# Long convolutions around a Haar perceptron layer: whole-width transfers, an earlier threshold, and C's start inside A's end

## The chip, the cores and the metric

The kernel runs on one core of a Trainium2 chip. The metric is the device time of one execution in microseconds; the kernel before took 3163.57 us (median of 3 runs, 3160.73 to 3165.43). The engines are PE (TensorE, matrix multiplication into PSUM), DVE (VectorE), ACT (ScalarE), POOL (GpSimd, which works on SBUF here) and SP (SyncE, whose queue issues every DMA of this kernel). Each engine works through its own queue in order, and waits on semaphores for the others.

## The reference, cut to what matters

The input `x` is 4 images of 64 channels of 256 x 256, in float32. Four layers follow one another:

```
x  = conv(x, filters of L0)        # two-dimensional causal long convolution, plus x * bias
f1 = haar2d(x)                     # all eight levels, along both axes
for i in 0, 1:
    f4   = einsum(f1 * v[i], conv_w[i])             # mixes the 64 channels, point by point
    acc += sign(f4) * relu(abs(f4) - tau[i])        # soft threshold
x  = haar2d_inverse(acc) + x
x  = conv(x, filters of L2)
x  = conv(x, filters of L3)
```

The filter of a convolution is the outer product of two filters of 256 taps, one along each axis, that a small network of sines makes. So a convolution is a multiplication with a triangular Toeplitz matrix along the rows and one along the columns.

## The kernel before, in words

**Three phases.** Phase A does the first convolution and the Haar transform, channel by channel. Phase B mixes the channels and applies the soft threshold, row of coefficients by row. Phase C undoes the transform and does the last two convolutions, again channel by channel. Between them the data lies in HBM: A writes `coef`, B reads it and writes `mixed`, C reads that. The four images are worked through as two groups of two. B of a group needs all channels of A; C of a group needs all rows of B.

**Phase A** has 32 rounds a group, each of two channels, so four images a round. A round has 12 pieces: four of `rows` (PE lines 223 and 224, then a copy on ACT, L292), four of `columns` (PE, then bias and addition on DVE, L302), and four of `product` for the round before (PE L317, the Haar transform along one axis, evicted by ACT, L325). The transform along the other axis is a row of small additions and subtractions on POOL (L241 and L244), of which two are issued with a piece. `coarsest` (L331 to L333) finishes two coefficients and `store` (L339) writes `coef`. Loads of `x` (L104) and of the Toeplitz matrices (L215) are issued two rounds ahead.

**Phase B** has 64 steps a group. A step is one row of each of the two halves of the 128 coefficient rows: 64 channels of one row on partitions 0 to 63, 64 channels of the other on partitions 64 to 127. `load` issues, for each half, one DMA for `f` (L392), one for `v` (L396) and one for `tau` (L397), each to 64 partitions; `store` (L455) writes each half with a DMA. In the first step of a group three DVE operations (L449 to L451) turn a pair of the first row into sum and difference. A step has two units `u`, one for each of the two terms of the sum. A unit does:

- `mix`: two multiplications of 128 x 512 on PE (L409) into a PSUM tile `f4`, of which there are two; `mix_sb` holds the channel weights twice, on its diagonal
- `multiply`: f4 times v, on DVE (L413)
- `sign` of f4 into an SBUF tile `m`, on ACT (L417), and `magnitude`, f4 = |f4|, on ACT (L420)
- `less`: f4 minus tau, on DVE (L424)
- `threshold`: max(f4, 0) times m, on DVE (L429)
- `add`: the even unit's term to `f` on POOL (L434), the odd unit's to that on POOL (L440) or, in every second step, on DVE (L438), which then reads f4

The pieces of B are written so that unit `u` and unit `u - 1` overlap: piece 0 has `mix(u)` and `less(u - 1)`; piece 1 has `multiply(u)`, `sign(u)`, then `threshold(u - 1)` and `add`; piece 2 has `magnitude(u)`.

**Phase C** has 32 rounds a group of 20 pieces: `product` (PE L522, ACT L526), `rows` and `columns` of two convolutions (PE lines 223 and 224, ACT L533, DVE L546). Before a round, POOL makes the inverse sums (L264 and L266) from the loaded `mixed`.

**The order of the work** is written out by hand: there is no scheduler, and instructions go into the queues in the order of the calls. `beside(main, side, lead, tail)` (L585) calls the pieces of `main` and spreads those of `side` evenly between them, from piece `lead` to `tail` pieces before the end. First A's first group runs with the filter network beside it; then A's second group with B's first (lead 20, tail 4), C's first group with B's second (lead 8, tail 40), and C's second group alone. C's round 0 loads, sums and filters are issued inside C's piece 0 (L559 to L564), after all of A.

Of the kernel before, what the change touches and what calls it, by code (L numbers as in the profile page):

```python
# [29 lines left out]
F32 = mybir.dt.float32  # L33
AF = mybir.ActivationFunctionType
ALU = mybir.AluOpType
# [30 lines left out]

@with_exitstack
def conv_haar_kernel(
    ctx: ExitStack, tc: tile.TileContext, x, zT, w1, wbd, cols, decay, bias, haarW, haarH, wcol, wrow, mixT, v, tau, out
):  # L70
    nc = tc.nc
    ctx.enter_context(tc.manual_schedule())
# [123 lines left out]
    bias_sb = const.tile([P, NL * C], F32, tag="bias", name="bias_sb")  # L196
    nc.sync.dma_start(bias_sb, bias.partition_broadcast(P))
    mix_sb = const.tile([P, 2, P], F32, tag="mix", name="mix_sb")
    nc.gpsimd.memset(mix_sb, 0.0)
    for i in range(2):  # L200
        for g in range(2):
            s = slice(g * C, (g + 1) * C)
            nc.sync.dma_start(mix_sb[s, i, s], mixT[i])

    def load_toeplitz(l, t, bufs):

# [68 lines left out]
    def phase_a():  # L275


        total = GROUPS * ROUNDS
        st = [dict() for _ in range(total + 1)]
        pieces = []  # L280

        def load(t):
            if t < total:
                st[t]["x"] = first_x[t] if t < len(first_x) else load_x(t)
                st[t]["toep"] = load_toeplitz(0, t, 4 * CI)

        def rows(t, n):
            s = st[t]
            ps = bank(f"a1ps{n}_{t}")
            toeplitz(ps, s["x"][:, 2 * n : 2 * n + 2], s["toep"][n // NB], 0)  # L290
            s["y", n] = image("t0", f"ay{n}_{t}")
            nc.scalar.copy(s["y", n], ps)  # L292

        def columns(t, n):
            s = st[t]
            c = t % ROUNDS * CI + n // NB
            if n == 0:
                s["x1"] = big("m0", f"x1_{t}", 2)
            ps = bank(f"a2ps{n}_{t}")
            toeplitz(ps, s["y", n], s["toep"][n // NB], 1)  # L300
            cut = slice(2 * n, 2 * n + 2)
            nc.vector.scalar_tensor_tensor(  # L302
                s["x1"][:, cut], s["x"][:, cut], bias_sb[:, c : c + 1], ps, ALU.mult, ALU.add
            )
            if n == M - 1:
                s["fw"] = big("m1", f"fw_{t}", 2)
                s["ops"] = forward_free(s["x1"], s["fw"], f"f{t}_")

        def product(t, j):
            s = st[t]  # L310
            n, m = j // 2 * 2, j % 2
            if j == 0:
                s["f"] = big("out", f"f_{t}", 2)
            ps = bank(f"a3ps{j}_{t}")
            for e in range(2):
                for k in range(2):
                    nc.tensor.matmul(  # L317
                        ps[:, e, bass.ts(k, P)],
                        s["fw"][:, 2 * (n + e) + k, bass.ts(m, P)],
                        haarH_sb[:, k, :],  # L320
                        start=True,
                        stop=True,
                    )
            f4 = s["f"].rearrange("p (n m) k -> p n m k", m=2)
            nc.scalar.activation(f4[:, n : n + 2, m, :], ps, AF.Copy, scale=wcol_sb[:, m : m + 1])  # L325

        def coarsest(t):

            pairs = st[t]["f"].rearrange("p n (h q) -> p n h q", h=2)[:, :, :, 0]
            sd = ac.tile([P, 2 * M, 2], F32, tag="sd", name=f"sd_{t}", bufs=2)  # L330
            nc.gpsimd.tensor_tensor(sd[:, :, 0], pairs[:, :, 0], pairs[:, :, 1], ALU.add)  # L331
            nc.gpsimd.tensor_tensor(sd[:, :, 1], pairs[:, :, 0], pairs[:, :, 1], ALU.subtract)
            nc.gpsimd.tensor_copy(pairs, sd)  # L333

        def store(t):
            grp, c0 = t // ROUNDS, t % ROUNDS * CI
            for e in range(CI):
                src = st[t]["f"][:, 2 * e * NB : 2 * (e + 1) * NB].rearrange("p (b h) k -> p b h k", h=2)
                nc.sync.dma_start(coef[grp][c0 + e], src)  # L339
            st[t].clear()  # L340

        def piece(t, j):
            now, last = t < total, t > 0
            if j == 0:
                if t == 0:
                    load(0)
                    load(1)
                load(t + 2)
            if j < M:
                if now:  # L350
                    rows(t, j)
                if last:
                    run(st[t - 1]["ops"], 2)
            elif j < 2 * M:
                if now:
                    columns(t, j - M)
                if j == M and t > 1:
                    coarsest(t - 2)
                if j == M + 2 and t > 1:
                    store(t - 2)  # L360
            else:
                if last:
                    product(t - 1, j - 2 * M)
                if now:
                    run(st[t]["ops"], 2)

        for t in range(total + 1):
            for j in range(3 * M):
                pieces.append(lambda t=t, j=j: piece(t, j))
        pieces.append(lambda: (coarsest(total - 1), store(total - 1)))  # L370
        return pieces

    def phase_b(grp):

# [5 lines left out]
        def load(s):  # L380
            if s >= STEPS:
                return
            d = st[s]
            r0 = s * ROWS
            d["f"] = bp.tile([P, ROWS, NB, W], F32, tag="ft", name=f"ft_{grp}_{s}", bufs=4)
            d["v"] = bp.tile([P, ROWS, 2, W], F32, tag="v", name=f"v_{grp}_{s}", bufs=3)
            d["tau"] = bp.tile([P, ROWS, 2, W], F32, tag="tau", name=f"tau_{grp}_{s}", bufs=3)
            for g in range(2):
                part = slice(g * C, (g + 1) * C)
                rows = slice(g * C + r0, g * C + r0 + ROWS)  # L390
                flat = lambda ap: ap.rearrange("r i h k -> (r i h k)").partition_broadcast(C)
                nc.sync.dma_start(  # L392
                    d["f"][part].rearrange("p r b w -> p (r b w)"),
                    coef[grp][:, rows].rearrange("c r b h k -> c (r b h k)"),
                )
                nc.sync.dma_start(d["v"][part].rearrange("p r i w -> p (r i w)"), flat(v[rows]))  # L396
                nc.sync.dma_start(d["tau"][part].rearrange("p r i w -> p (r i w)"), flat(taus[rows]))  # L397

        def data(t):
            return t.rearrange("p r b w -> p (r b) w")  # L400
# [41 lines left out]
        def store(s):  # L442
            r0 = s * ROWS
            gt = st[s]["g"]
            if r0 == 0:

                top = gt[:C, 0].rearrange("p b (h k) -> p b h k", h=2)
                sd = bp.tile([C, NB, 2, N], F32, tag="sd", name=f"sd_{grp}", bufs=1)
                nc.vector.tensor_tensor(sd[:, :, 0, :], top[:, :, 0, :], top[:, :, 1, :], ALU.add)  # L449
                nc.vector.tensor_tensor(sd[:, :, 1, :], top[:, :, 0, :], top[:, :, 1, :], ALU.subtract)  # L450
                nc.vector.tensor_copy(top, sd)  # L451
            for g in range(2):
                part = slice(g * C, (g + 1) * C)
                rows = slice(g * C + r0, g * C + r0 + ROWS)
                nc.sync.dma_start(  # L455
                    mixed[grp][:, rows].rearrange("c r b h k -> c (r b h k)"), gt[part].rearrange("p r b w -> p (r b w)")
                )
            st[s].clear()

        def piece(u, j):  # L460
            s, i = divmod(u, 2)
            if j == 0:
                if u < units:
                    mix(u)
                if 0 < u <= units:
                    less(u - 1)
            elif j == 1:
                if u < units:
                    multiply(u)
                    sign(u)  # L470
                if 0 < u <= units:
                    threshold(u - 1)
                    add((u - 1) // 2, 1 - i)
                if i == 0 and s >= 2:
                    store(s - 2)
                    load(s + 2)
            elif u < units:
                magnitude(u)
# [11 lines left out]
    def phase_c():  # L490
# [65 lines left out]
        def piece(t, j):  # L556
            stage, n = divmod(j, M)
            if j == 0:
                if t == 0:  # L559
                    load(0)  # L560
                    load(1)
                    sums(0)
                    run(st[0]["ops"], 16)
                    filters(0)  # L564
                filters(t + 1)
                load(t + 2)
                sums(t + 1)
# [8 lines left out]
            if t + 1 < total:  # L576
                run(st[t + 1]["ops"], 1)

        for t in range(total):
            for j in range(5 * M):  # L580
                pieces.append(lambda t=t, j=j: piece(t, j))
        pieces.append(lambda: store(total - 1))
        return pieces

    def beside(main, side, lead, tail):  # L585

# [5 lines left out]
                q()  # L592
            done = max(done, want)

    a, c = phase_a(), phase_c()
    cut_a, cut_c = ROUNDS * 3 * M, ROUNDS * 5 * M
    beside(a[:cut_a], rest, 2, 3 * M)
    early.close()
    bp = pool("b", 2)
    bps = pool("bps", 2, space=PSUM)  # L600
    beside(a[cut_a:], phase_b(0), 5 * M, M)
    beside(c[:cut_c], phase_b(1), 2 * M, 10 * M)
    beside(c[cut_c:], [], 0, 0)


# [99 lines left out]
```

## Time and profile before

| | |
|---|---|
| median of 3 runs | 3163.57 us |
| profiled execution | 3161.11 us, its span 3159.3 us |
| PE | 2973.0 us, 94% of the span |
| DVE | 1564.9 us, 50% |
| ACT | 1230.2 us, 39% |
| POOL | 1817.4 us, 58% |
| DMA, all queues | 656.76 MB, mean 208 GB/s |
| granted PE clock | 0.989 |

The profile is of one execution. Its span goes from the first instruction to the last. A row of its windows gives the busy time of each engine in a stretch of the span, with the number of instructions in brackets. A row of its waits gives the waiting instruction, what released it, the idle time in total, how often, and the longest. A row of its timeline gives start, duration, engine, line, operation, the tile written and the tiles read, and in brackets the idle time before it with what ended it. B's first multiply starts at 533.3 us, the last of its first group at 1306.15, C's first product at 1342.91, and B's last multiply near 2300.6. A's rounds without B beside them are 14.06 us apart (products at 506.35 and 520.41), and C's without B 24.53 us.

### The profile page before, as it was taken

To read this page: it belongs to the slowest core of one execution; us is meant where nothing else is said; L and a number is where in the kernel's file an instruction comes from. 1 tells how busy PE (TensorE), PEld (TensorE's weight loads), DVE (VectorE), ACT (ScalarE), POOL (GpSimd) and SP (SyncE) were. 2 spreads that over 40 slices of the span, in tenths; PEclk is the share of its full clock that TensorE was granted. 3 is DMA by queue.
4 is the path that set the end of the run, shared out by engine and by line. 5 is a ranking of instruction groups with operands and counts; after the bars stand their busy time and mean duration, and the time that the engine had idled before them with its cause. 6 is when DMAs were issued, how large, how long until landed. Compare 5 with 4: busy or idle time off the path is not lost. (4 is left out here: it accounts for less than half of the span.)

```text
span 3159.3 us, 48195 instructions
## 1 busy us (share of the span) xinstructions
PE 2973.0 (94%) x17432; PEld 2535.1 (80%) x17432; DVE 1564.9 (50%) x1657; ACT 1230.2 (39%) x1799; POOL 1817.4 (58%) x2437
## 2 busy tenths in 40 slices
PE   5999999888988888599999999999999999999999
PEld 5989997666666666488877878887899999999998
DVE  2232213777777777457666667666732222222222
ACT  1333333444544445344444444444432222232222
POOL 2776675666766766655556555565664444444441
PEclk9999999999999999899999999999999999999999
DMA  6857898999999999789888988989744444444442
GB/s 159 215 179 193 226 234 226 258 274 272 274 275 270 274 277 265 230 195 268 233 244 226 250 231 238 249 226 255 205 141 132 141 124 124 124 138 132 127 120 87
DMA packets 380227, 656.76 MB, mean 208 GB/s; under 512 B 42134, under 2 KB 281399, under 8 KB 379992
## 3 DMA queue, kind: packets, MB, share of 16 engines
q1 hardware_dynamic: 379992, 653.69, 76.6%
q8 instruction: 140, 2.29, 0.3%
q14 instruction: 95, 0.78, 0.1%
HBM read 438.10 MB, written 215.42 MB: 207 GB/s over the span
## 5 line engine op out<-in xcount | busy, mean ns | idle before, releaser
L409 PE MATMUL f<-ft,mix_sb 128*128 128x512 f32 x1024 | 506.1, 617 | 112.6 <-DVE gt L438 57.3
L434 POOL TENSOR_TENSOR m<-m,ft 128x1024 f32<-128x1024 f32 x128 | 301.7, 2357 | 453.1 <-DVE m L429 441.4
L417 ACT ACTIVATE m<-f 128x1024 f32<-128x1024 f32 x256 | 262.5, 1025 | 513.1 <-DVE f L413 504.3
L546 DVE SCALAR_TENSOR_TENSOR cy<-cz,bias_sb,c1c 128x512 f32<-128x512 f32 x256 | 189.2, 746 | 515.9 <-PE c1c L224 515.9
L424 DVE TENSOR_TENSOR f<-f,tau 128x1024 f32<-128x1024 f32 x256 | 314.6, 1229 | 197.0 <-ACT f L420 194.2
L302 DVE SCALAR_TENSOR_TENSOR x<-x,bias_sb,a2ps 128x512 f32<-128x512 f32 x256 | 189.0, 745 | 428.8 <-PE a2ps L224 380.4
L409 PEld LDWEIGHTS f<-ft,mix_sb 128*128 128x128 f32 x1024 | 177.5, 193 | 258.3 <-issue 142.6
L546 DVE SCALAR_TENSOR_TENSOR o<-cy,bias_sb,c2c 128x512 f32<-128x512 f32 x256 | 189.5, 746 | 348.7 <-PE c2c L224 348.7
L413 DVE TENSOR_TENSOR f<-f,v 128x1024 f32<-128x1024 f32 x256 | 313.8, 1226 | 54.9 <-PE f L409 51.8
L223 PE MATMUL a1ps<-toep,x 128*128 128x256 f32 x1024 | 310.1, 385 | 21.3 <-DMA toep<-filt 18.1
L223 PE MATMUL a2ps<-toep,ay 128*128 128x256 f32 x1024 | 305.9, 381 | 1.8 <-ACT ay L292 1.8
L223 PE MATMUL c2r<-toep,cy 128*128 128x256 f32 x1024 | 305.8, 380 | 0.3 <-DVE cy L546 0.3
L223 PE MATMUL c1c<-toep,ch 128*128 128x256 f32 x1024 | 305.8, 380 | 0.0
L223 PE MATMUL c1r<-toep,cz 128*128 128x256 f32 x1024 | 305.8, 380 | 0.0
L223 PE MATMUL c2c<-toep,ch 128*128 128x256 f32 x1024 | 305.8, 380 | 0.0
L533 ACT COPY ch<-c2r 128x512 f32<-128x512 f32 x256 | 149.4, 588 | 382.4 <-PE c2r L224 382.2
L325 ACT ACTIVATE f<-a3ps,wcol_sb 128x512 f32<-128x512 f32 x256 | 175.7, 686 | 293.2 <-PE a3ps L317 251.5
L317 PEld LDWEIGHTS a3ps<-haarH_sb,fw 128*128 128x128 f32 x2048 | 244.9, 195 | 32.5 <-issue 22.7
L526 ACT COPY cz<-c1ps 128x512 f32<-128x512 f32 x256 | 148.1, 588 | 309.5 <-PE c1ps L522 309.5
L522 PEld LDWEIGHTS c1ps<-haarW_sb,ci 128*128 128x128 f32 x2048 | 238.8, 193 | 36.6 <-POOL ci L266 24.4
L522 PE MATMUL c1ps<-haarW_sb,ci 128*128 128x128 f32 x2048 | 244.6, 276 | 23.4 <-POOL ci L266 23.3
L420 ACT ACTIVATE f<-f 128x1024 f32<-128x1024 f32 x256 | 263.9, 1031 | 0.0
(64 smaller groups left out, 5868.5 us busy)
## 6 DMA issues: line engine op xcount, KB each, us to landing
toep<-filt SPq DMA_DIRECT2D x768, 128.0 KB, 4.1
x<-in_x SPq DMA_DIRECT2D x256, 256.0 KB, 7.8
coef<-f SPq DMA_DIRECT2D x128, 512.0 KB, 7.3
ft<-coef SPq DMA_DIRECT2D x256, 256.0 KB, 6.6
v<-in_v SPq DMA_DIRECT2D x256, 256.0 KB, 7.0
tau<-taus SPq DMA_DIRECT2D x256, 256.0 KB, 7.0
mixed<-gt SPq DMA_DIRECT2D x256, 256.0 KB, 6.0
g<-mixed SPq DMA_DIRECT2D x128, 512.0 KB, 5.4
```

The source lines that it names most:

```text
L223: nc.tensor.matmul(ps[:, m, :], data[:, 0, cut], t[:, which, :], start=True, stop=False)
L302: nc.vector.scalar_tensor_tensor(s["x1"][:, cut], s["x"][:, cut], bias_sb[:, c : c + 1], ps, ALU.mult, ALU.add)
L317: nc.tensor.matmul(ps[:, e, bass.ts(k, P)], s["fw"][:, 2 * (n + e) + k, bass.ts(m, P)], haarH_sb[:, k, :], start=True, stop=True,)
L325: nc.scalar.activation(f4[:, n : n + 2, m, :], ps, AF.Copy, scale=wcol_sb[:, m : m + 1])
L409: nc.tensor.matmul(un[u]["f4"][:, j, :], mix_sb[:, u % 2, :], f[:, j, :], start=True, stop=True)
L413: nc.vector.tensor_tensor(f4, f4, weights(st[u // 2]["v"], u % 2), ALU.mult)
L417: nc.scalar.activation(un[u]["m"], un[u]["f4"], AF.Sign)
L420: nc.scalar.activation(un[u]["f4"], un[u]["f4"], AF.Abs)
L424: nc.vector.tensor_tensor(f4, f4, weights(st[u // 2]["tau"], u % 2), ALU.subtract)
L434: nc.gpsimd.tensor_tensor(m0, m0, data(st[s]["f"]), ALU.add)
L522: nc.tensor.matmul(ps[:, m, bass.ts(h, P)], s["ci"][:, 2 * n + h, bass.ts(m, P)], haarW_sb, start=True, stop=True)
L546: nc.vector.scalar_tensor_tensor(o, s["y", n], bias_sb[:, at : at + 1], ps, ALU.mult, ALU.add)
```

## The change

There are four edits.

1. Each step of B loads `f`, `v` and `tau` and stores its result with one DMA over all 128 partitions, in place of one per half. For that the two halves are interleaved: partition 2c + g holds channel c of half g. `mix_sb` is laid out accordingly by the host and loaded whole, without a memset. The first row of a group is now on every second partition, so its three operations run on all partitions, with a factor (`first_sb`) that is 1 and -1, or 0 and 1, by partition.
2. In a unit of B, `threshold(u - 1)` and `add` stand right behind `less(u - 1)` in piece 0, so in front of `multiply(u)` in DVE's queue; before they stood behind it.
3. A's last round is taken out of its list: the products of the last round, with what POOL still has to do for them, form `a_last`, whose four products are placed between the first four `rows` of C.
4. B's first group is spread over A's second group up to six stages (24 pieces) before its end, where it went on to the end before. C's loads, filters and first sums of round 0 are issued in those 24 pieces. B's second group starts at piece 20 of the list that C leads, where it was piece 8.

```diff
-            for g in range(2):
-                part = slice(g * C, (g + 1) * C)
-                rows = slice(g * C + r0, g * C + r0 + ROWS)
-                flat = lambda ap: ap.rearrange("r i h k -> (r i h k)").partition_broadcast(C)
-                nc.sync.dma_start(
-                    d["f"][part].rearrange("p r b w -> p (r b w)"),
-                    coef[grp][:, rows].rearrange("c r b h k -> c (r b h k)"),
-                )
-                nc.sync.dma_start(d["v"][part].rearrange("p r i w -> p (r i w)"), flat(v[rows]))
-                nc.sync.dma_start(d["tau"][part].rearrange("p r i w -> p (r i w)"), flat(taus[rows]))
+            nc.sync.dma_start(d["f"].rearrange("p r b w -> p (r b w)"), rows_of(coef[grp], r0))
+            for name, src in (("v", v), ("tau", taus)):
+
+                flat = bass.AP(src.tensor, src.offset + r0 * 2 * W, [[0, C], [C * 2 * W, 2], [1, ROWS * 2 * W]])
+                nc.sync.dma_start(d[name].rearrange("p r i w -> p (r i w)"), flat)
+
+        def rows_of(ap, r0):
+            return ap.rearrange("c (g r) b h k -> c g r (b h k)", g=2)[:, :, r0 : r0 + ROWS].rearrange(
+                "c g r e -> c g (r e)"
+            )
...
-            for g in range(2):
-                part = slice(g * C, (g + 1) * C)
-                rows = slice(g * C + r0, g * C + r0 + ROWS)
-                nc.sync.dma_start(
-                    mixed[grp][:, rows].rearrange("c r b h k -> c (r b h k)"), gt[part].rearrange("p r b w -> p (r b w)")
-                )
+                top, low = (gt[:, 0].rearrange("p b (h k) -> p b h k", h=2)[:, :, h, :] for h in range(2))
+                d = bp.tile([P, NB, N], F32, tag="sd", name=f"sd_{grp}", bufs=1)
+                one, sign_ = first_sb[:, 0:1], first_sb[:, 1:2]
+                nc.vector.tensor_scalar(d, top, one, None, ALU.mult)
+                nc.vector.scalar_tensor_tensor(top, low, one, top, ALU.mult, ALU.add)
+                nc.vector.scalar_tensor_tensor(low, low, sign_, d, ALU.mult, ALU.add)
+            nc.sync.dma_start(rows_of(mixed[grp], r0), gt.rearrange("p r b w -> p (r b w)"))
...
                 if 0 < u <= units:
                     less(u - 1)
+                    threshold(u - 1)
+                    add((u - 1) // 2, 1 - i)
             elif j == 1:
                 if u < units:
                     multiply(u)
                     sign(u)
-                if 0 < u <= units:
-                    threshold(u - 1)
-                    add((u - 1) // 2, 1 - i)
...
-        for t in range(total + 1):
+        for t in range(total):
             for j in range(3 * M):
                 pieces.append(lambda t=t, j=j: piece(t, j))
-        pieces.append(lambda: (coarsest(total - 1), store(total - 1)))
-        return pieces
+        t = total - 1
+        last = [lambda: (coarsest(t - 1), store(t - 1), run(st[t]["ops"], 16))]
+        last += [lambda j=j: product(t, j) for j in range(M)]
+        last.append(lambda: (coarsest(t), store(t)))
+        return pieces, last
...
+        def start():
+            load(0)
+            load(1)
+            filters(0)
+            sums(0)
+
+        first = [start] + [lambda: run(st[0]["ops"], 2)] * 8
...
-    beside(a[cut_a:], phase_b(0), 5 * M, M)
-    beside(c[:cut_c], phase_b(1), 2 * M, 10 * M)
+    beside(a[cut_a : -6 * M], phase_b(0), 5 * M, 0)
+    beside(a[-6 * M : -2 * M], c_first[:1], 2 * M, M)
+    beside(a[-2 * M :], c_first[1:], 0, 0)
+    main = a_last[:1] + c[:M]
+    for pair in zip(c[M : 2 * M], a_last[1:]):
+        main += pair
+    main += a_last[M + 1 :] + c[2 * M : cut_c]
+    beside(main, phase_b(1), 5 * M, 10 * M)
     beside(c[cut_c:], [], 0, 0)
```

More of the change, by code (lines that the diff above doesn't have):

```diff
@@ L68, in conv_haar_kernel @@
 def conv_haar_kernel(
-    ctx: ExitStack, tc: tile.TileContext, x, zT, w1, wbd, cols, decay, bias, haarW, haarH, wcol, wrow, mixT, v, tau, out
+    ctx: ExitStack, tc: tile.TileContext, x, zT, w1, wbd, cols, decay, bias, haarW, haarH, wcol, wrow, mixT, first, v, tau, out
 ):
@@ L198, in conv_haar_kernel @@
     mix_sb = const.tile([P, 2, P], F32, tag="mix", name="mix_sb")
-    nc.gpsimd.memset(mix_sb, 0.0)
-    for i in range(2):
-        for g in range(2):
-            s = slice(g * C, (g + 1) * C)
-            nc.sync.dma_start(mix_sb[s, i, s], mixT[i])
+    nc.sync.dma_start(mix_sb, mixT)
+    first_sb = const.tile([P, 2], F32, tag="first", name="first_sb")
+    nc.sync.dma_start(first_sb, first)
     def load_toeplitz(l, t, bufs):
@@ L342, in piece @@
         def piece(t, j):
-            now, last = t < total, t > 0
             if j == 0:
@@ L349, in piece @@
             if j < M:
-                if now:
-                    rows(t, j)
-                if last:
+                rows(t, j)
+                if t > 0:
                     run(st[t - 1]["ops"], 2)
             elif j < 2 * M:
-                if now:
-                    columns(t, j - M)
+                columns(t, j - M)
                 if j == M and t > 1:
@@ L361, in piece @@
             else:
-                if last:
+                if t > 0:
                     product(t - 1, j - 2 * M)
-                if now:
+                if t < total - 1:
                     run(st[t]["ops"], 2)
-        for t in range(total + 1):
+        for t in range(total):
             for j in range(3 * M):
                 pieces.append(lambda t=t, j=j: piece(t, j))
-        pieces.append(lambda: (coarsest(total - 1), store(total - 1)))
-        return pieces
+        t = total - 1
[3 more added lines that the diff above has]
+        return pieces, last
     def phase_b(grp):
@@ L445, in store @@
             if r0 == 0:
[L447 to L452, printed above, removed]
-                part = slice(g * C, (g + 1) * C)
-                rows = slice(g * C + r0, g * C + r0 + ROWS)
-                nc.sync.dma_start(
-                    mixed[grp][:, rows].rearrange("c r b h k -> c (r b h k)"), gt[part].rearrange("p r b w -> p (r b w)")
-                )
+                top, low = (gt[:, 0].rearrange("p b (h k) -> p b h k", h=2)[:, :, h, :] for h in range(2))
[5 more added lines that the diff above has]
+            nc.sync.dma_start(rows_of(mixed[grp], r0), gt.rearrange("p r b w -> p (r b w)"))
             st[s].clear()
@@ L558, in piece @@
             if j == 0:
[L559 to L564, printed above, removed]
                 filters(t + 1)
@@ L582, in phase_c @@
         pieces.append(lambda: store(total - 1))
-        return pieces
+        return first, pieces
     def beside(main, side, lead, tail):
@@ L593, in beside @@
             done = max(done, want)
-    a, c = phase_a(), phase_c()
+    (a, a_last), (c_first, c) = phase_a(), phase_c()
     cut_a, cut_c = ROUNDS * 3 * M, ROUNDS * 5 * M
@@ L662 @@
     haarW[0] *= math.sqrt(0.5)
+    mix = np.zeros((C, 2, 2, C, 2), np.float32)
+    for g in range(2):
+        mix[:, g, :, :, g] = a["L1_conv_conv_w"].transpose(2, 0, 1)
+    odd = np.arange(P) % 2
     arrays = {
@@ L690 @@
         "wrow": f(w[order].astype(np.float32)),
-        "mixT": f(a["L1_conv_conv_w"].transpose(0, 2, 1)),
+        "mixT": f(mix.reshape(P, 2, P)),
+        "first": f(np.stack([1.0 - odd, 2.0 * odd - 1.0], axis=1).astype(np.float32)),
         "v": by_row(v),
```

## The prediction

> **What bounds the kernel now.** I read the page first, then the busy time by stage (cut where B's first and last multiply and C's first product stand), then the waits of the stage that runs A beside B, then the timeline of a few units of B.
>
> ```profile
> span 3159.3 us, 48195 instructions
> PE 2973.0 (94%) x17432; PEld 2535.1 (80%) x17432; DVE 1564.9 (50%) x1657; ACT 1230.2 (39%) x1799; POOL 1817.4 (58%) x2437
> ```
>
> TensorE is busy for 94%, so only its idle 186 us can be won. The columns below are: stretch, length, busy time of PE, PEld, DVE, ACT, POOL, granted clock, DMA share, GB/s.
>
> ```profile
> 57.00:506.00 449.00, 443.64 (x3013) 416.38 (x3012) 113.03 (x155) 158.89 (x251) 319.83 (x601) 1.00 0.79 213
> 533.00:1306.00 773.00, 679.35 (x3403) 509.83 (x3402) 568.01 (x534) 378.69 (x495) 513.89 (x655) 0.98 1.03 268
> 1306.00:1343.00 37.00, 5.98 (x38) 5.60 (x36) 6.18 (x6) 5.38 (x7) 21.72 (x40) 0.63 0.69 215
> 1343.00:2302.00 959.00, 945.59 (x5196) 770.16 (x5197) 648.40 (x648) 428.53 (x607) 550.47 (x564) 1.00 0.87 234
> 2302.00:3159.00 857.00, 853.39 (x5559) 795.86 (x5557) 213.33 (x284) 245.01 (x418) 386.48 (x540) 1.00 0.43 126
> ```
>
> PE idles 94 us where A runs beside B's first half, 31 us in the turn to C, 13 us where C runs beside B's second half. The DMA share of 1.03 says that the 16 engines never rest in the A+B stage. Do compute engines wait for them? The waits of 533 to 1306:
>
> ```profile
> ACT m L417 <- DVE f L413: 218.4, 59, 7.4
> DVE f L424 <- ACT f L420: 100.1, 79, 3.1
> ...
> PE f L409 <- DVE gt L438: 47.7, 30, 3.5
> ...
> DVE f L413 <- PE f L409: 38.1, 27, 12.0
> ...
> PE f L409 <- DVE m L429: 37.4, 38, 2.7
> ```
>
> PE's idle time there is 85 us in front of the mix (L409), for the threshold (L429) or the add after it (L438), which still read the PSUM tile that the mix of two units later writes. PE waits only 4.2 us for ft's DMA. So the stage is set by B's handoffs between PE, DVE and ACT. Here are two of its units, in the timeline:
>
> ```profile
> 1305.01 1.23 DVE L424 TENSOR_TENSOR f<-f,tau 128x1024 f32<-128x1024 f32 x1 [1.46 <-ACT f L420]
> ...
> 1306.15 1.22 DVE L413 TENSOR_TENSOR f<-f,v 128x1024 f32<-128x1024 f32 x1
> ...
> 1307.46 1.02 ACT L417 ACTIVATE m<-f 128x1024 f32<-128x1024 f32 x1 [0.26 <-DVE f L413]
> ...
> 1308.38 1.02 ACT L420 ACTIVATE f<-f 128x1024 f32<-128x1024 f32 x1
> ...
> 1309.44 1.23 DVE L424 TENSOR_TENSOR f<-f,tau 128x1024 f32<-128x1024 f32 x1 [0.94 <-ACT f L420]
> ...
> 1310.70 1.23 DVE L429 SCALAR_TENSOR_TENSOR f<-f,m 128x1024 f32<-128x1024 f32 x1
> ```
>
> The reader should see a closed ring: subtract (L424), multiply of the next unit (L413), its sign (L417), its magnitude (L420), its subtract. Start to start it takes 1.14 + 1.31 + 0.92 + 1.06 = 4.43 us. The threshold (L429) normally follows the multiply, outside this ring; only the last unit shows it right behind its own subtract, 1.26 us later.
>
> **What the skill says.** "DMA: Bandwidth & Descriptors", section "Rules for kernel authors", says that two transfers to disjoint partition halves serialize and that one over 128 partitions should be used; "SBUF — State Buffer", section "Door 1: The DMA port swizzle", gives 196 GB/s for 64 partitions and 328 for 128 at 1 MiB. The trace fits (268 GB/s at a full share with B's halves among the traffic) but doesn't isolate them. "VectorE: DVE Perf Modes", section "The DRAIN you can't avoid", says that a Vector instruction which reads its predecessor's result still needs a semaphore. The trace agrees: 1.13 us from multiply to an independent threshold, 1.26 from a subtract to its own threshold, 1.31 from a threshold to the add that reads it (1021.61 to 1022.92).
>
> **The change, part by part.** The sum is against the profiled span, 3159.3 us; that execution took 3161.1, and the median of the runs is 3163.57, 4.3 over the span.
>
> 1. Threshold in front of the multiply, A+B stage. Now first multiply to last is 773 us for 127 steps, 6.09 us a unit. The new queue on DVE is subtract(u), threshold(u), add, multiply(u+1). The threshold and every add on DVE move into the ring, since the multiply, and so sign, magnitude and the next subtract, are queued behind them. Per unit: subtract to threshold 1.26; threshold to multiply 1.13; multiply to sign 1.31; sign to magnitude 0.92; magnitude to subtract 1.06: 5.68. A quarter of the units have the DVE add: 1.31 / 4 = 0.33. That gives 6.01. Then comes A's work that stands inside the ring. In the built program's order, 54 of L302 stand between threshold or add and multiply in B's 128 units, at 0.66 us start to start: 0.28. And 74 of A's ACT evictions stand between sign and magnitude, at 0.46 (L292) or 0.57 (L325): 0.30. Total 6.59 us. All are ready in time, because PE runs ahead: its own need per unit is 2.6 pieces of A at 1.17 (products 14.06 us apart, 12 pieces) plus 2.0 for a mix, 5.06. So (6.59 - 6.09) x 127 = **+64**. PE's wait at the mix grows to about 1.5 us a unit, with the threshold named again: the tile is free early in the ring, but the ring comes round late. Bounds: 6.01 if nothing inserted counts (-10), 6.8 with stray waits (+90).
>
> 2. Turn to C. B is packed into 340 pieces of A instead of 373, so about 34 pieces of A (40 us of PE) and 4 products (3.6) now follow B's last mix; before, only a few products did. From B's last multiply to C's first product was 36.8 us, mostly idle. Now PE works 40 us there; the first sums on POOL (11.8 us from 1331.08 to 1342.9) run beside the last 8 pieces (9.4 us), so some 3 us stay open. A's last products follow, behind a transform on POOL (some 9.6 us of operations from 1301.24 on) that is queued behind those sums: 3.6 us of work and some 4 of wait. So C stands 40 + 3 + 7 - 37 = **+13** later relative to B's end. The idle time is filled, but with A work that used to fit beside B for nothing. Its cover is a ring slower than PE; if the ring were PE's pace, each of the 34 pieces would have saved 1.17. B's second half starts six pieces (7 us) after A's last store is issued; store and load take 3 to 4 and 6 to 7 us: **+3**.
>
> 3. Threshold order, C+B stage. PE's need per unit is 4.45 pieces of C at 1.227 (a round is 24.53 us in the chain, 20 pieces) plus 1.72 and a bubble: 7.3 us; multiplies are 7.40 apart now. The ring here is 6.01 + 0.38 (0.58 of L546 per unit at 0.66) + 0.41 (0.88 copies at 0.46) = 6.80, below PE. PE's waits for L438 and L429 here, 9.6 + 2.1 us, can go; copies queued behind a later sign may cost some of it back. I take **-3**, from -12 to +15, because the margin is half a microsecond.
>
> 4. Transfers. Per step of two units, 8 DMAs of 256 KB become 4 of 512 KB. SP issues of about 0.59 us each fall by 2.4 us a step. Even at the 268 GB/s of now, a unit of the ring needs 1.05 MB for B and 0.57 MB for A (2.6 of 12 pieces of 2.6 MB), 6.0 us, under 6.59; at the 411 GB/s seen in the turn to C it is 3.9. Nothing waits for it: **0**. Were they slower than now by over a tenth, they would set the stage.
>
> 5. Small edits. Five start instructions become two loads, behind PE's wait of 18 us for toep: 0. The first rows' three DVE operations took 1.5 + 1.55 + 0.9; new ones of 128x512 near 0.75 each: -2 at most per half, taken as -1 in all.
>
> Sum: 64 + 13 + 3 - 3 - 1 = +76, so a span of 3235 and a median of **3240 us**, 2.4% slower.
>
> **Rivals.**
> - *The waits just vanish* (faster). PE's 85 us at L409 are waits for exactly the instruction that is moved forward. If the ring overlapped so that PE set the pace at 5.06: -131 + 13 + 3 - 4, near 3045. Against it: sign reads what multiply writes and subtract reads what magnitude writes, in order on both engines. It decides at ring = 5.98 us; below that the kernel gains.
> - *A's inserted work falls outside the ring.* Then the ring is 6.01: -10 + 13 + 3 - 4 = +2, 3166. For it: ACT is busy half of the stage. Against: the inserts stand between two ring members in the queue and cost their spacing in the traced units.
> - *C+B turns over as well.* Its margin is 0.5 us and units with an add take 1 more; at 7.65 a unit it would be +35, near 3278. For it: ACT already waits 286 us for multiplies in that stage. Against: PE's tile is free some 4 us ahead.
> - *Transfers were the bound and get quicker*, SP's queue being full in the A+B stage. With the ring as the new floor this gives the same 3240; if instead the new shape were slower, over 3300.
>
> **How the numbers follow.** Ring at 6.4 to 6.8, C+B near even: 0.67, its own range 3215 to 3265. C+B too: 0.13. Inserts outside, or partly: 0.11. Waits vanish: 0.06. Slow transfers: 0.03. Leaving out the waits that vanish, half of the third case and the slow transfers, the range is 3170 to 3295. Within 0.2% (6 us, about what a measurement can tell) takes 0.05 out of the third case; faster takes the fourth and 0.01; slower the rest.
>
> **What will show it.** First multiply to last in the A+B stage near 837 us; threshold 1.26 behind its subtract; PE's idle at L409 near 195 us there; a DMA share clearly under 1; PE idle in the turn under 15 us; the C+B multiplies about 7.3 apart. I am wrong if the multiplies of the first half are under 6.0 apart (a step of the ring overlaps), or if a DMA is named in front of mix or multiply.

## The result and the profile after

The changed kernel took 3204.16 us (3202.0 to 3207.26) where the kernel before took 3162.15 us on the same chip: a ratio of 1.0133, with a 95% interval of 1.0115 to 1.0151. It is slower by 42 us, where +76 was forecast: faster than the 3215 to 3265 us of the prediction's main case, and inside its wide range of 3170 to 3295.

The page of the changed kernel, and then its busy time by stage, cut at the same events as before (B's first and last multiply of the first half, C's first product, B's last multiply). Columns: stretch, length, PE, PEld, DVE, ACT, POOL, clock, DMA share, GB/s.

```profile
span 3201.6 us, 47458 instructions
PE 3004.2 (94%) x17432; PEld 2551.8 (80%) x17432; DVE 1580.0 (49%) x1657; ACT 1234.4 (39%) x1799; POOL 1817.5 (57%) x2436
```

```profile
57.00:506.00 449.00, 443.62 (x3006) 416.18 (x3005) 112.67 (x154) 158.83 (x251) 317.31 (x595) 1.00 0.77 213
527.00:1355.00 828.00, 683.28 (x3164) 496.24 (x3163) 567.78 (x524) 368.81 (x476) 493.07 (x617) 0.93 0.73 248
1355.00:1396.00 41.00, 35.01 (x240) 32.42 (x238) 13.41 (x16) 14.87 (x22) 34.07 (x60) 0.97 0.47 167
1396.00:2346.00 950.00, 946.17 (x5238) 775.17 (x5239) 655.78 (x648) 433.83 (x612) 562.20 (x587) 1.00 0.71 242
2346.00:3201.00 855.00, 851.81 (x5547) 794.24 (x5545) 213.06 (x284) 244.41 (x417) 385.88 (x541) 1.00 0.42 125
```

The A+B stage grew from 773 to 828 us, and PE is idle there for 145 us, not 94. The turn to C has 6 us of idle PE in place of 31. The C+B stage shrank from 959 to 950 us and PE idles 4 us in it, not 13. The DMA share of the A+B stage fell from 1.03 to 0.73. The span's +42.2 us is made of four parts: B's first multiply comes 6.6 us earlier (526.7 for 533.3), A+B from first to last multiply takes 55.4 us more (828.2 for 772.8), the way from there to C's first product 4.7 more (41.5 for 36.8), and from that product to the end 11.3 less (1805.1 for 1816.4).

The waits of the A+B stage in the changed kernel (waiting instruction, releaser, total us, times, longest):

```profile
ACT m L417 <- DVE f L413: 419.3, 123, 5.8
DVE f L424 <- ACT f L420: 249.0, 125, 2.8
...
PE f L409 <- DVE gt L438: 75.8, 29, 4.5
...
PE f L409 <- DVE m L429: 68.6, 52, 3.2
...
DVE f L413 <- PE f L409: 6.4, 1, 6.4
```

DVE and ACT now wait for each other in nearly every one of the 128 units (123 and 125 times; before 59 and 79), and the multiply no longer waits for PE except once, at the start. So the ring of DVE and ACT runs on its own, and PE waits for it. PE's waits at the mix (L409), which the earlier threshold was to shorten, rose from 85 to 144 us.

The timeline of VectorE, and then of ScalarE, in two units of the changed kernel:

```profile
1006.64 1.23 DVE L424 TENSOR_TENSOR f<-f,tau 128x1024 f32<-128x1024 f32 x1 [2.66 <-ACT f L420]
1007.91 1.23 DVE L429 SCALAR_TENSOR_TENSOR m<-f,m 128x1024 f32<-128x1024 f32 x1
1009.05 1.22 DVE L413 TENSOR_TENSOR f<-f,v 128x1024 f32<-128x1024 f32 x1
1012.86 1.23 DVE L424 TENSOR_TENSOR f<-f,tau 128x1024 f32<-128x1024 f32 x1 [2.58 <-ACT f L420]
```

```profile
1010.31 1.02 ACT L417 ACTIVATE m<-f 128x1024 f32<-128x1024 f32 x1 [2.52 <-DVE f L413]
1011.23 0.68 ACT L325 ACTIVATE f<-a3ps,wcol_sb 128x512 f32<-128x512 f32 x1
1011.80 1.03 ACT L420 ACTIVATE f<-f 128x1024 f32<-128x1024 f32 x1
```

Subtract at 1006.64, threshold 1.27 later, multiply 1.14 later, sign 1.26 later, then one of A's evictions and the magnitude, 1.49 together, and the next subtract 1.06 after that: 6.22 us, in which DVE idles 2.58 in front of the subtract and ACT 2.52 in front of the sign. Over all units of the first half, the A+B step (the mean distance from one multiply to the next) is 6.52 us; it was 6.09. In the second half, the C+B step is 7.18 us; it was 7.40.

### The profile page after: what moved, and what is told of

The parts are those of the page before. It is cut to its first block, busy times and chain, and to the rows that moved or that the text cites. A ratio compares the mean times of both kernels' runs of the same rounds, so it can differ in the third digit from the quotient of the medians.

```text
span 3201.6 us, 47458 instructions
## 1 busy us (share of the span) xinstructions
PE 3004.2 (94%) x17432; PEld 2551.8 (80%) x17432; DVE 1580.0 (49%) x1657; ACT 1234.4 (39%) x1799; POOL 1817.5 (57%) x2436
## 4 chain that ended last, share of the span: by engine, by line
PE 70%; DVE 12%; ACT 6%; issue 3%; POOL 2%; DMA 1%; SPq 0%; ACTq 0%; DVEq 0%; POOLq 0%
PE f L409 9%; PE c1ps L517 7%; PE c2r L223 7%; PE c2c L223 7%; PE c1c L223 7%; PE c1r L223 7%; DVE f L424 4%; PE c2c L224 4%; PE c2r L224 4%; PE c1c L224 4%; PE c1r L224 4%; DVE f L413 3%; PE a1ps L223 3%; ACT f L420 3%; PE a3ps L317 3%; PE a2ps L223 3%
## 5 line engine op out<-in xcount | busy, mean ns | idle before, releaser
L409 PE MATMUL f<-ft,mix_sb 128*128 128x512 f32 x1024 | 527.3, 640 | 148.1 <-DVE gt L438 75.8
L409 PEld LDWEIGHTS f<-ft,mix_sb 128*128 128x128 f32 x1024 | 182.9, 199 | 297.3 <-issue 131.9
L302 DVE SCALAR_TENSOR_TENSOR x<-x,bias_sb,a2ps 128x512 f32<-128x512 f32 x256 | 188.4, 744 | 382.1 <-PE a2ps L224 341.8
L223 PE MATMUL a1ps<-toep,x 128*128 128x256 f32 x1024 | 316.7, 392 | 20.0 <-DMA toep<-filt 16.7
L317 PE MATMUL a3ps<-haarH_sb,fw 128*128 128x128 f32 x2048 | 251.9, 279 | 4.9 <-POOL fw L235 4.9
```

What stands on the lines that cost most here:

```text
L223: nc.tensor.matmul(ps[:, m, :], data[:, 0, cut], t[:, which, :], start=True, stop=False)
L302: nc.vector.scalar_tensor_tensor(s["x1"][:, cut], s["x"][:, cut], bias_sb[:, c : c + 1], ps, ALU.mult, ALU.add)
L317: nc.tensor.matmul(ps[:, e, bass.ts(k, P)], s["fw"][:, 2 * (n + e) + k, bass.ts(m, P)], haarH_sb[:, k, :], start=True, stop=True,)
L409: nc.tensor.matmul(un[u]["f4"][:, j, :], mix_sb[:, u % 2, :], f[:, j, :], start=True, stop=True)
```

## The experiments

The times of an experiment are compared with the kernel before on the same chip. On the three chips that served for them the kernel before took 3174 us. Its profile, though, is from another chip, where it took 3161 us: a stage of an experiment that is set against a stage of the kernel before is compared across chips, and some of the difference can be the chip's.

**E1, the order alone.** In the kernel before:

```diff
                     less(u - 1)
+                    threshold(u - 1)
+                    add((u - 1) // 2, 1 - i)
             elif j == 1:
...
                     sign(u)
-                if 0 < u <= units:
-                    threshold(u - 1)
-                    add((u - 1) // 2, 1 - i)
```

> The kernel before with the threshold and the add placed in front of the next multiply, and nothing else. Ring theory: the multiplies of A+B stand 5.68 + 0.33 (adds) + 0.22 (L302 in the ring) + 0.32 (evictions between sign and magnitude) = 6.55 us apart (6.09 before), +59 us; C+B loses its waits at the mix, 7.40 to about 7.27, -16 us; total near 3205 us. Rival, the turn or the packing of B costs the time of the changed kernel: 3165 us or less here, and multiplies not above 6.1 apart.

Measured: 3203.56 us, ratio 1.0091 (1.0076 to 1.0106). The A+B multiplies are 6.571 us apart, the C+B ones 7.257. Its A+B and C+B stages:

```profile
535.00:1369.00 834.00, 699.85 (x3402) 519.98 (x3401) 575.58 (x536) 378.71 (x496) 516.78 (x657) 0.96 0.94 249
...
1405.00:2345.00 940.00, 939.47 (x5197) 769.13 (x5198) 655.59 (x648) 430.36 (x607) 550.97 (x564) 1.00 0.88 239
```

The ring's sum was right to 0.02 us in the first stage, and the expected step of the second to 0.01. Against the profile of the kernel before, this one edit costs 61 us where B's handoffs set the pace, and wins 19 where PE does: PE is idle for half a microsecond in 940, where it was 13.4 in 959. The order alone gives the changed kernel's time (3203.6 and 3204.2 us); the turn and the packing aren't needed for the loss. On E1's own chip the edit costs 29 us and not 61 - 19 = 42, because the kernel before is 12 us slower there. In which stage these 12 us lie is not shown.

**E2, the transfers alone.** The kernel before with the changed `load`, `store` and `mix_sb`, the old order and the old placing.

> The kernel before with B's transfers as single DMAs over 128 partitions, and nothing else. Ring theory (engines hand over to each other, transfers are hidden): multiplies of A+B still 6.0 to 6.1 apart, the first of them some 6 us earlier because fewer DMAs stand in front of it; total 3150 to 3163 us. Rival, SP's full queue paced the stage: 5.9 or less apart, total under 3140 us.

Measured: 3147.37 us, ratio 0.9914 (0.9898 to 0.9931). The A+B step is 5.995 us, C+B 7.402, and the first multiply stands at 527.2. Its A+B stage:

```profile
533.00:1288.00 755.00, 665.02 (x3360) 501.36 (x3359) 563.38 (x532) 374.98 (x490) 513.26 (x655) 0.99 0.80 272
```

On this chip that is 27 us less than the kernel before. Against the profile of the kernel before it is 18 us (spans of 3159.3 and 3141.1): 6.2 us at the start, 11.4 in the A+B stage, 0.9 in the turn. That is neither theory whole: the step lies at the edge of what the ring theory has, and yet the total is below its 3150. The same traffic takes a share of 0.80 of the DMA engines, not 1.03, at 272 GB/s.

**E3 and E4, the turn, with the old transfers and with the new ones.** E3 is the kernel before with the changed lists of A and C and the four `beside` lines. E4 is the changed kernel with the old order:

```diff
                     less(u - 1)
-                    threshold(u - 1)
-                    add((u - 1) // 2, 1 - i)
             elif j == 1:
...
                     sign(u)
+                if 0 < u <= units:
+                    threshold(u - 1)
+                    add((u - 1) // 2, 1 - i)
```

> The kernel before with B packed into fewer pieces of A and C's start inside A's end, and nothing else. Ring theory: with 2.6 pieces of A per unit for 2.85 the old order's step falls by up to 0.25 x 1.17 = 0.29 to about 5.8 us, -36 us, and the turn itself costs +6 and fills about 25 us of idle time with A's pieces: near 3135 us. Rival, the DMA engines at 268 GB/s and a full share allow no less than 6.0 us a unit: the step stays at 6.0 or above, DMA waits appear in front of mix or multiply, and the total is near 3160 us.

> The changed kernel with the threshold put back behind the multiply: single DMAs and the turn alone. Ring theory: A+B step about 5.8 us (6.52 in the changed kernel), C+B step about 7.3 (7.18), so near 3125 us, under both kernels. Rival, the single DMAs or the turn carry the loss: 3165 us or more. If the DMAs limited the run of the turn alone, this one is faster than that by 15 us or more; if not, by about 6.

Measured: E3 3173.0 us, ratio 0.9993 (0.9987 to 1.0000); E4 3147.28 us, ratio 0.9915 (0.9900 to 0.9930). The A+B steps are 5.988 and 5.843. The A+B stages of E3 and of E4:

```profile
535.00:1296.00 761.00, 650.89 (x3147) 479.97 (x3146) 560.51 (x523) 367.54 (x475) 490.52 (x608) 0.97 1.04 268
```

```profile
529.00:1271.00 742.00, 641.83 (x3144) 475.41 (x3144) 558.72 (x523) 367.87 (x475) 491.09 (x612) 0.98 0.80 275
```

E3 stands at a full DMA share and at the 6.0 us that this rate allows, and E4, on the same chip, which differs from it in the transfers and what belongs to them, is 0.145 us a unit faster: 18 us in this stage. So in the old order the transfers do hold this stage, as the rival said, though the total of 3173 us is under neither theory's figure. The waits of the compute engines show little of it. E3's waits of PE at the mix, by releaser:

```profile
PE f L410 <- DVE gt L439: 50.3, 28, 3.5
PE f L410 <- DVE m L430: 42.4, 44, 2.2
PE f L410 <- DMA ft<-coef: 11.0, 4, 4.9
```

Eleven microseconds name a DMA; the same view of E4 has none for it. The queue that issues the transfers shows the rest. The longest waits of SP between 600 and 1250 us, of E3 and then of E4:

```profile
SPq L216 <- DMA tau<-taus: 33.8, 47, 1.1
SPq L398 <- DMA coef<-f: 23.6, 23, 1.6
```

```profile
SPq L392 <- DVE f L424: 111.8, 48, 4.3
SPq L339 <- POOL f L333: 72.9, 16, 10.4
```

With the halves 253 of SP's 281 us of waits name a DMA, an earlier transfer that had to land first. With single transfers it is 41 of 388; SP then waits for the engines to free a tile or to finish a result.

E4 beside E2 prices the turn: 3147.3 and 3147.4 us, nothing. Its parts by the events: the A+B step falls by 0.15 us (-19 us over 127 units), the way to C's first product grows by 7.7 (35.9 to 43.6), and from there to the end by 11.8 (1816.6 to 1828.4). The turn and the C+B stage of E2, and then of E4:

```profile
1288.00:1324.00 36.00, 6.25 (x40) 5.87 (x39) 6.59 (x6) 5.38 (x7) 21.60 (x38) 0.63 0.66 219
1324.00:2283.00 959.00, 945.12 (x5190) 769.96 (x5191) 647.65 (x647) 428.31 (x606) 550.55 (x564) 1.00 0.68 234
```

```profile
1271.00:1314.00 43.00, 37.79 (x261) 35.38 (x259) 14.47 (x17) 15.36 (x23) 34.62 (x63) 0.98 0.48 172
1314.00:2284.00 970.00, 951.02 (x5217) 775.26 (x5218) 645.76 (x646) 431.64 (x610) 560.76 (x584) 1.00 0.69 235
```

PE's idle time in the turn falls from 30 to 5 us, and grows by 5 in the C+B stage, where PE also works 6 us longer. In the A+B stage the A pieces that were taken from beside B gave back only 0.15 of the 0.29 us of PE time that they hold per unit.

The edits don't add up. In the old order the single transfers are worth 26 us (E3 to E4); in the new order they and the turn together are worth nothing (E1's 3203.6 us, and 3204.2 for the changed kernel). So the order costs 29 us with the halves and the old placing (E1), and 57 with single transfers and the turn (E4 to the changed kernel, which takes 3204 and 3205 us on the two chips that ran it). What the transfers alone are worth in the new order was not run.

**E5 and E6, the ring shortened in two places.** Both start from the changed kernel. E5:

```diff
                     sign(u)
+                    magnitude(u)
...
-            elif u < units:
-                magnitude(u)
```

E6:

```diff
-            o = un[u]["f4"] if u % 4 == 3 else un[u]["m"]
+            o = un[u]["m"]
...
-                if s % 2:
-                    nc.vector.tensor_tensor(data(st[s]["g"]), m0, un[2 * s + 1]["f4"], ALU.add)
-                else:
-                    nc.gpsimd.tensor_tensor(data(st[s]["g"]), m0, un[2 * s + 1]["m"], ALU.add)
+                nc.gpsimd.tensor_tensor(data(st[s]["g"]), m0, un[2 * s + 1]["m"], ALU.add)
```

> The changed kernel with the magnitude issued right behind its sign, so that no eviction of A or C stands between them on ACT. Ring theory: sign to magnitude falls from 1.22 to 0.92 us, the A+B step from 6.52 to about 6.22, -38 us; C+B is set by PE and stays near 7.18; total about 3166 us, or 1.2% under the changed kernel. Rival, something else than the ring paces A+B (PE, the DMAs): step and total within 8 us of the changed kernel.

> The changed kernel with the last add of every step on POOL, none on DVE. Ring theory: the adds leave the ring, 0.25 x 1.31 = 0.33 us a unit, so the A+B step is about 6.19 us, -42 us, total about 3162 us. Rival, POOL takes over (each step then has two operations of 2.36 us beside A's and C's sums): the step stays above 6.4 and waits for POOL appear in front of A's products.

Measured: E5 3167.21 us, ratio 0.9977 (0.9970 to 0.9984), A+B step 6.215. E6 3170.08 us, ratio 0.9987 (0.9980 to 0.9994), step 6.235. ScalarE's timeline in E5 shows what was taken out:

```profile
1006.58 1.02 ACT L417 ACTIVATE m<-f 128x1024 f32<-128x1024 f32 x1 [3.76 <-DVE f L413]
1007.50 1.02 ACT L420 ACTIVATE f<-f 128x1024 f32<-128x1024 f32 x1
1008.44 0.67 ACT L325 ACTIVATE f<-a3ps,wcol_sb 128x512 f32<-128x512 f32 x1
```

The eviction now stands behind the magnitude, sign to magnitude is 0.92 us in every unit, and the step falls by 0.31 us, where 0.30 was expected. In E6 it falls by 0.29, where 0.33 was expected. Nothing in E5 makes less work on any engine: only the order of two operations on ACT is changed. So the A+B step is the sum of what stands in the ring, on DVE and on ACT, and neither PE nor the DMA engines nor POOL paced this stage of the changed kernel. The C+B step, which PE sets, stays near 7.19 us in both.

**E7 and E8, a better kernel.** E7 is the changed kernel with the order chosen by the stage; E8 adds the edit of E6 to it.

```diff
-                    threshold(u - 1)
-                    add((u - 1) // 2, 1 - i)
+                    if grp == 1:
+                        threshold(u - 1)
+                        add((u - 1) // 2, 1 - i)
             elif j == 1:
...
                     sign(u)
+                if grp == 0 and 0 < u <= units:
+                    threshold(u - 1)
+                    add((u - 1) // 2, 1 - i)
```

> The changed kernel with the old order in B's first half and the new one in its second. If the two stages take the edit with opposite signs: A+B step 5.84 as with the old order, C+B step 7.18 as in the changed kernel, total 3147 - 19 = about 3128 us, under every kernel so far. Rival, the C+B gain of the changed kernel came from the turn or the transfers: C+B at 7.35 or total at 3145 us or more.

> The kernel with the order by half, and the last add of every step on POOL. In the old order PE's mix waits 56 us for the add on DVE, which reads the tile that the mix needs; on POOL it reads SBUF alone. Theory: up to 0.25 x 1.31 = 0.33 us off the A+B step, to about 5.55, and 0 in C+B: near 3092 us. Rival, the threshold in front of it is the wait that remains: the step stays above 5.75, total above 3115 us.

Measured: E7 3124.41 us, ratio 0.9840 (0.9825 to 0.9855), steps 5.869 and 7.181. E8 3079.07 us, ratio 0.9701 (0.9685 to 0.9718), steps 5.490 and 7.194. The A+B stage of E8:

```profile
527.00:1224.00 697.00, 627.67 (x3130) 466.96 (x3129) 522.71 (x492) 368.05 (x475) 559.24 (x641) 0.99 0.85 293
```

E7 confirms that the two stages take the order with opposite signs. E8's gain of 0.38 us a unit is over the 0.33 that was expected at most, and its total 13 us under the expected one, so that theory isn't the whole of it; PE idles 69 us in the stage, POOL is busy for 80% of it. Both beat the kernel before and the changed one.

**E9 to E11.** E9 adds E5's edit to E8. E10 is E8 without the turn: the kernel before's lists and `beside` lines. E11 is the changed kernel once more.

> The kernel with the order by half and the adds on POOL, and the magnitude right behind its sign in both halves. If the old order's A+B step (5.49) is still partly the ring of subtract, multiply, sign and magnitude, whose inserted evictions cost 0.30 a unit, it falls to about 5.3, -25 us. If PE (5.06 a unit) and its wait for the threshold pace it, it stays within 0.1, total within 10 us of 3079.

> The same as the order by half with the adds on POOL, but with the kernel before's placing: B's first half spread to the end of A, C's start after A. With the old order and DVE adds the turn was worth nothing (3147.4 without, 3147.3 with). If that is because B's handoffs and not PE set the A+B step, the turn should be worth more here, where the step is nearer to PE's need: 3090 to 3105 us. If the turn is worth nothing whatever the step, 3079 within 6 us.

> The changed kernel on the chip of the other runs, where the kernel before takes 3174 us and not 3162. The ring doesn't depend on the DMA engines, so the changed kernel should take 3204 us again and its loss against the kernel before be 0.9% here; were the whole chip slower, it would take about 3216.

Measured: E9 3066.62 us, ratio 0.9666 (0.9649 to 0.9682), A+B step 5.395. E10 3079.82 us, ratio 0.9705 (0.9690 to 0.9719), step 5.623. E11 3205.17 us, ratio 1.0101 (1.0086 to 1.0116), step 6.532. E9 is the fastest kernel of the study; its step fell by 0.095, between the two expectations, so in the old order the ring is only part of what paces the stage. Of E10's two readings the second came: the turn is worth nothing here as well, though the step is nearer to PE's need. Its parts, from E10 to E8, are those of E2 to E4 again: 17 us less in the A+B stage (714.2 to 697.2), 5.8 more to C's first product, 11.1 more from there to the end. Beside B, PE works 34 us less with the turn and idles 17 more (52 to 69), so half of what was taken away came back as idle time. Why the parts balance so exactly stays open. E11 fits: the changed kernel takes the same time on a chip where the kernel before is 12 us slower. So the size of the loss, 1.0 to 1.3%, moves with the kernel before, not with the changed one. Why the kernel before differs between chips stays open.

## Why the prediction was right or wrong

**The mechanism was right.** Step 1, the ring, was put at 6.59 us and is 6.52. Its links were read right: 1.27 for 1.26 from subtract to threshold, 1.31 from multiply to sign, 1.22 from sign to magnitude, 1.06 to the next subtract. One term was mis-sized: 54 of L302 were counted between threshold or add and multiply, 0.28 us a unit. The trace has 37 there in the 127 gaps between multiplies, 0.29 per unit, so 0.29 x 0.66 = 0.19 us, and the ring comes to 6.50. The stage grew by 55 us where +64 was forecast. PE's wait at the mix, forecast near 195 us, is 144, because PE's need was mis-sized too: PE is busy for 5.4 us a unit in this stage and not for 5.06, at a granted clock of 0.93.

**Step 4, the transfers at nothing, missed the start.** "Nothing waits for it: 0" holds for the stage, where the ring hides the transfers. But the first multiply comes 6.6 us earlier, because the first loads land sooner (E4's is 6.4 earlier than E3's, on one chip). With the old order it would be wrong: there the transfers are worth 18 us of the stage (E3 to E4). The waits of its compute engines named DMAs for hardly anything, and the prediction took that for proof. A DMA share of 1.03, together with SP's own waits, was the better sign: between 600 and 1250 us of the kernel before, 249 of 279 us of these name a DMA. It was left to a rival whose worth was put at the floor of the ring alone. The 411 GB/s set against it is the peak of one slice of under 2 us; the mean of that view is 226.

**Step 3, C+B at -3, was mis-sized.** The order alone is worth -19 there (1816.4 to 1797.3 from C's first product to the end, E1), beyond the -12 that was its bound. The prediction's own PE need without its bubble, 4.45 x 1.227 + 1.72, is 7.18, and 7.18 is what the changed kernel shows. So the terms that failed are the bubble of some 0.1 us a unit, and the guess that copies would cost part of the gain back. PE's waits named in the view made 11.7 us; the idle time of the stage fell by 12.9, and PE's busy time by another 6, for a reason that isn't shown. The ring of 6.80 that was worked out for this stage didn't bind, as the prediction said: the step is what PE needs, 7.26 in E1 and 7.18 with fewer pieces of C per unit.

**Step 2, the turn.** C's first product is 41.5 us behind B's last multiply, 43 forecast; its open waits are 5.2 us at the product and 3.5 at A's last products, where 3 and 4 were written. PE doesn't wait for the first load of B's second half. From C's first product on, the turn's own price is +11.8 in E4, near the +10 that follows from the prediction's 7 and 3. Its make-up is not quite the forecast's: PE works 6 us longer there and idles 5, of which 3 are the wait at A's last products.

Together: start -7, ring -9, turn -1, C -17, which is the gap between +76 and +42. All four point the same way.

**The rivals.** "The waits just vanish" is out: the step rose, and shrinking the ring in two places moved it by about the sums (E5, E6). "A's inserted work falls outside the ring" is out by E5: moving the evictions, 74 in 128 units, out of it is worth 0.31 us a unit. "C+B turns over as well" is out: that stage got faster. "Transfers were the bound" was half right, for the old order and not for the changed kernel.

One rival is not in the prediction: a slower TensorE clock. In the A+B stage the granted clock fell from 0.98 to 0.93, and PE was busy for 683 us with 3164 matmuls, where E4 needs 642 for 3144 at 0.98. But the multiply waits for PE only once in the stage. E11, the same kernel, had 0.95 there, and its step was no shorter (6.532 us). Why the clock fell isn't shown. The stage in E11:

```profile
529.00:1358.00 829.00, 675.42 (x3163) 492.13 (x3163) 567.34 (x523) 368.34 (x476) 492.37 (x615) 0.95 0.73 247
```

## What to carry to other kernels

An edit of the order of two instructions on one engine is to be judged by the rings it lengthens: list who waits for whom until the list closes, add the start-to-start times, include what stands between in each queue, and compare with the busiest engine's need per turn. The same edit can be right in one stage and wrong in the next; here PE needs 5.1 to 5.4 us a unit beside A and 7.2 beside C, the new ring takes 6.5 beside A, and choosing the order by stage gave more than either order throughout. Pieces that stand in a ring for no reason, here an add that POOL can do and an eviction between sign and magnitude, are worth about their spacing times the number of turns, as long as the ring sets the pace: 0.29 and 0.31 us a unit in E6 and E5. Where it sets the pace only in part, the same move of the magnitude gave 0.095 (E9).

## What the runs showed of the hardware

The first loads of B's first half show both shapes of a transfer; in both kernels the last issues before them are two stores of `coef`, 4 us ahead. In the kernel before, the issues of the first `ft` halves, and the mix that waits for both:

```profile
522.01 0.48 SPq L392 DMA_DIRECT2D ft<-coef  x1
...
523.81 0.59 SPq L392 DMA_DIRECT2D ft<-coef  x1
...
529.53 3.75 PE L409 MATMUL f<-ft,mix_sb 128*128 128x512 f32 x4 [7.17 <-DMA ft<-coef]
```

In the changed kernel:

```profile
521.00 0.32 SPq L388 DMA_DIRECT2D ft<-coef  x1
...
524.70 1.98 PE L409 MATMUL f<-ft,mix_sb 128*128 128x512 f32 x4 [3.37 <-DMA ft<-coef]
```

The same 512 KB are there 3.7 us after the first issue as one transfer over 128 partitions, and 7.5 us as two over 64, with two other loads issued between them (5.7 us after the second issue). The first six issues of loads on SP's queue took 0.32 to 0.61 us each for 512 KB in the changed kernel, and 0.48 to 0.60 for 256 KB in the kernel before, so an issue of twice the bytes took no longer. In the A+B stage of the old order the single transfers need a share of 0.80 of the DMA engines at 272 GB/s, the halves 1.03 at 268 (E2 and the kernel before): at the same rate the halves kept the engines busy for longer.

A stage was slowed by its transfers while the waits of its compute engines named few of them: 0.145 us a unit, 18 us, between E3 and E4, with 11 us of PE's waits under a DMA's name. The issuing queue's own waits told the two apart: 253 of 281 us name a DMA in E3, 41 of 388 in E4.
